# Values of the first group of heads for the last two token blocks by Strassen's scheme

## The chip, the cores and the metric

The kernel runs on one core of a Trainium2 chip. The metric is the device time of one execution in microseconds (us). TensorE does the matrix products, VectorE (DVE in the profile) and ScalarE (ACT) the elementwise work, GpSimd (POOL) and SyncE (SP) mostly issue transfers. Everything is float32.

## The reference

One transformer block over 2048 tokens of width 512, with modulation vectors made from a conditioning row `c`:

```
mod = silu(c) @ wmod                      # sa, ca, ga, sb, cb, gb, each 512 wide
h   = layernorm(x) * (1 + ca) + sa
q, k, v = h @ Q_w + Q_b, h @ K_w + K_b, h @ V_w + V_b      # 16 heads of 128
scores  = softmax(causal(q @ k.T / sqrt(128)))
x   = x + ga * ((scores @ v) @ O_w + O_b)
h   = layernorm(x) * (1 + cb) + sb
x   = x + gb * (top-4-of-64 expert FFN(h) + 2 shared experts(h))
```

Only the product `h @ V_w` is touched here, for heads 0 and 1 and for tokens 1024 to 2047.

## The kernel before

**Layout.** The normalised tokens are kept transposed in four blocks of 512 tokens, `hTs[0]` to `hTs[3]`, each 128 partitions x 4 chunks of the width x 512 tokens. For each pair of blocks `b` there are four differences of their halves, `Ts[b]`, made once by `sum_h(b)` on VectorE. They serve a scheme of Strassen's kind (seven products in place of eight) that already makes the queries and keys of heads 1 to 15 (`project`) and the values of head groups 1 to 7 (`values`, L434 to L487). A head group is two heads; group 0 is heads 0 and 1.

**Two ways to make values.** `make_v(g, t)` (L489 to L504) makes the values of both heads of a group for one tile of 128 tokens: four matmuls with 256 moving columns into one PSUM tile, tag "mm", and one ScalarE copy out of it (L504). Eight such calls make two token blocks. `values(g, b, s)` makes the same two token blocks in seven steps. Each step is one product of eight matmuls with 128 moving columns (four token tiles, two chunks of the width, L447) into one PSUM tile of the same tag, and one or two evictions: the first product goes by a ScalarE copy (L461) into a buffer `p_`, and the others are added into `u` or into the value tiles by VectorE (L464 to L483, seven additions, the fourth step having two). The scheme needs sums of the group's weights, which `value_sums(g)` writes into `sgb` by four VectorE additions of 128x256 (L428 to L431). The tag "mm" has two PSUM buffers, so a product can begin when the eviction of the last but one is done.

A matmul of the source is two TensorE instructions in the profile, so a call of `make_v` shows as 8 instructions of 256 columns and a product of `values` as 16 of 128 columns, each with a weight load of 128x128 beside it (PEld).

**Order.** The attention runs as a list of steps (head, batch); each head has five batches of pairs of token tiles, `BATCHES = ((7,), (6,), (5, 0), (4, 1), (3, 2))`. For a batch, `softmax_work` gives chunks of up to 1024 keys: matmuls into `ps` (L572), a causal mask (L584) and the row maximum (L585, L589) on VectorE, the exponential on ScalarE (L591, L601), and a scaling by the row sums (L550 to L554 on VectorE, then L559 or L795). `swap` sends the probabilities through 16 transfers issued by SP (L616), `turn` transposes 32x32 blocks on VectorE (L626, four per batch), and `weighted_values` multiplies with the values (L644).

Ahead of the loop over the steps there is a prologue (L818 to L826), which has no `weighted_values` yet. It merges the softmax chunks of the first two batches of head 0 with other products as filler: the values of group 0 and the last three query blocks of head 0 (`plain`, L170, evicted by ScalarE at L177). The helper `merge(streams, marks)` writes the engines' instructions in an order fixed at build time: it always takes the next item from the stream that is least advanced by its share of columns, and calls a mark's function when the given share of all columns is done. Each engine then runs its own list in that order.

```python
work = softmax_work(0) + softmax_work(1)
fill = [(1024, lambda t=t: make_v(0, t)) for t in range(NT)]
fill += [(2048, lambda j=j: plain(0, j, qts[0, j])) for j in (2, 0, 1)]
merge([work[:4], fill[:8]], [])
swap(0)
marks = [(at, lambda a=a: turn(0, a)) for a, at in enumerate((0.55, 0.65, 0.75, 0.85))]
merge([work[4:], fill[8:]], marks)
swap(1)
```

In what follows, chunks 1 to 4 are those of the first batch (pair 7) and chunks 5 to 8 those of the second (pair 6).

Of the kernel before, what the change touches and what calls it, by code (L numbers as in the profile page):

```python
# [23 lines left out]
def adaln_block_kernel(  # L24
# [30 lines left out]
    NT = N // P  # L55
# [22 lines left out]
    sgb = const.tile([P, 2, D], F32)  # L78
# [6 lines left out]
    def merge(streams, marks):  # L85


        totals = [sum(c for c, _ in s) for s in streams]
        whole = sum(totals)
        done = [0] * len(streams)  # L90
        at = [0] * len(streams)
        marks = sorted(marks, key=lambda m: m[0])
        while True:
            ready = [i for i, s in enumerate(streams) if at[i] < len(s)]
            while marks and (not ready or sum(done) >= marks[0][0] * whole):
                marks.pop(0)[1]()
            if not ready:
                break
            i = min(ready, key=lambda i: (done[i] / totals[i], i))
            c, f = streams[i][at[i]]  # L100
            f()
            done[i] += c
            at[i] += 1
# [19 lines left out]
    with ExitStack() as att:  # L123
# [41 lines left out]
        def plain(b, j, dst):  # L165

            w = heads[0][b]
            ps = psA.tile([P, 512], F32, name="pqk", tag="mm")
            for k in range(DC):
                nc.tensor.matmul(  # L170
                    out=ps,
                    lhsT=w[:, k, :],
                    rhs=hTs[j][:, k, :],
                    start=(k == 0),
                    stop=(k == DC - 1),
                )
            nc.scalar.activation(  # L177
                dst, ps, AF.Identity, bias=qkb[:, b, 0:1], scale=scale if b == 0 else 1.0
            )
# [245 lines left out]
        def value_sums(g):  # L425
            wv = groups[g]
            s = sgb.rearrange("p a (j k d) -> p (a j) k d", j=2, k=2)
            nc.vector.tensor_add(s[:, 0], wv[:, 0:2, 1], wv[:, 2:4, 1])  # L428
            nc.vector.tensor_sub(s[:, 1], s[:, 0], wv[:, 0:2, 0])
            nc.vector.tensor_sub(s[:, 2], wv[:, 0:2, 0], wv[:, 0:2, 1])  # L430
            nc.vector.tensor_sub(s[:, 3], wv[:, 2:4, 0], s[:, 1])  # L431
            return s
# [56 lines left out]
        def make_v(g, t):  # L489

            if t % 4 == 0:
                at = vplace[g][t // 4]
                vts[g, t // 4] = vp.tile([P, 4, HG * DH], F32, name=f"v{at}")
            wv = groups[g]
            ps = psA.tile([P, HG * DH], F32, name="pv", tag="mm")
            for k in range(DC):
                nc.tensor.matmul(  # L497
                    out=ps,
                    lhsT=hTs[t // 4][:, k, (t % 4) * P : (t % 4 + 1) * P],
                    rhs=wv[:, k].rearrange("p i d -> p (i d)"),  # L500
                    start=(k == 0),
                    stop=(k == DC - 1),
                )
            nc.scalar.copy(vts[g, t // 4][:, t % 4, :], ps)  # L504
# [295 lines left out]
        def softmax_work(n):  # L800
            hd, s = steps[n]
            probs[n] = pp.tile([P, PW], F32, name="p")
            tiles = {}
            for pr, i, _ in CHUNKS[s]:
                if (pr, i) not in tiles:
                    tiles[pr, i] = softmax_tile(hd, s, pr, i, probs[n])
            assert sum(len(chunks) for chunks in tiles.values()) == len(CHUNKS[s])
            return [tiles[pr, i][c] for pr, i, c in CHUNKS[s]]

        def swap(n):  # L810
            flush()
            flush_shares()
            turned[n] = swap_blocks(steps[n][1], probs.pop(n))

        def turn(n, a):
            turn_blocks(steps[n][1], turned[n], a)

        with tc.manual_schedule():  # L818
            work = softmax_work(0) + softmax_work(1)
            fill = [(1024, lambda t=t: make_v(0, t)) for t in range(NT)]  # L820
            fill += [(2048, lambda j=j: plain(0, j, qts[0, j])) for j in (2, 0, 1)]
            merge([work[:4], fill[:8]], [])
            swap(0)
            marks = [(at, lambda a=a: turn(0, a)) for a, at in enumerate((0.55, 0.65, 0.75, 0.85))]
            merge([work[4:], fill[8:]], marks)
            swap(1)  # L826
            outs = []
            for n, (hd, s) in enumerate(steps):
                if s == 3:
                    if hd + 2 < H:  # L830
                        heads[hd + 2] = load_head(hd + 2)
                    if hd % HG == 1 and hd // HG + 2 < NG:
                        groups[hd // HG + 2] = load_group(hd // HG + 2)
                fill = fillers(hd, s)
                if (hd, s) in MOD_LOADS:
                    load_mod(MOD_LOADS[hd, s], hd // HG)
                if (hd, s) in MOD_ROWS:
                    fill.append((2048, lambda m=MOD_ROWS[hd, s]: late_mod(*m)))
                if (hd, s) in ((2, 3), (15, 2)):
                    mag = qkw.tile([P, 512], F32, name="p_")  # L840
                    gate(mag, ga if hd == 2 else gb)
                if (hd, s) == (14, 0):
                    nc.sync.dma_start(out=sgb, in_=modd.partition_broadcast(P))
                if (hd, s) == (14, 1):
                    fill.insert(2, (0, lambda: load_wo(0)))
                if (hd, s) == (14, 2):
                    load_wo(1)
                    load_ab(0, heads=((0, 4), (4, 8)))
                if (hd, s) == (14, 3):
                    load_wo(2)  # L850
                    load_ab(0, heads=((8, 12), (12, 14)))
                    first, second = [
                        vow.tile([P, DC, HG, DH], F32, name="wv").rearrange("p k i d -> p (k i d)")
                        for _ in range(2)
                    ]
                    parts += [first[:, :D], first[:, D:], second[:, :D]]
                    last3 = second[:, D : D + (NE - 1) * P]
                if (hd, s) == (14, 4):
                    load_wo(3)
                    load_ab(0, heads=((14, 15),))  # L860
                    for u in range(NE):
                        load_x_tile(u)
                    rest = spare(hd // HG)
                    nc.sync.dma_start(out=rest[0][:, :D], in_=O_b.partition_broadcast(P))
                    for u in range(NE):
                        outs += begin_output(u)
                if hd == H - 1 and s == 0:
                    load_ab(1, heads=((0, 4), (4, 8)))
                if hd == H - 1 and s == 1:
                    load_ab(1, heads=((8, 12), (12, 15)))  # L870
                if hd == H - 1 and s == 2:
                    load_ab(2)
                if hd == H - 1 and s == 4:
                    nc.vector.tensor_copy(ga, rest[0][:, D:])
                    nc.sync.dma_start(out=last3, in_=atd[H - 1, :, : (NE - 1) * P])
                    nc.sync.dma_start(out=ones, in_=atd[H - 1, :, (NE - 1) * P : NE * P])
                if outs:
                    upto = 8 if hd < H - 1 else (14, 14, 14, 10)[s]
                    fill += outs[:upto]
                    del outs[:upto]  # L880
                streams = [fill, weighted_values(hd, s, turned.pop(n))]
                if n + 2 < len(steps):
                    streams.insert(0, softmax_work(n + 2))
                marks = [(f, lambda i=i: scale_wo(i)) for f, i in WO_SCALES.get((hd, s), ())]
                if s == 4 and hd + 2 < H:
                    marks.append((0.05, lambda: scale_w(hd + 2)))
                    marks.append((0.3, lambda: sum_w(hd + 2)))
                if n + 1 < len(steps):
                    for a, at in enumerate((0.58, 0.66, 0.8, 0.88)):
                        marks.append((at, lambda a=a: turn(n + 1, a)))  # L890
                merge([st for st in streams if st], marks)
                if n + 2 < len(steps):
                    swap(n + 2)
            assert not outs and not ahead
# [273 lines left out]
    with ExitStack() as ex:  # L1168
# [346 lines left out]
        with tc.manual_schedule():  # L1515
# [13 lines left out]
            for n, (_, f) in enumerate(tail):  # L1529
                f()  # L1530
                upto = min(NT, READY[n])
                while done < upto:
                    t = order[done]
# [37 lines left out]
```

## Time and profile before

| | us |
|---|---|
| median of 3 runs | 2372.84 (2370.08 to 2377.7) |
| the profiled execution's own time | 2360.04 |
| its span, first to last instruction | 2358.2 |
| mean granted TensorE clock | 0.998 of full speed |

The profile and the trace are of that one execution, whose span leaves 1.8 us of its time around it. It ran 12.8 us faster than the median of the runs that are timed, so a sum of durations is compared with its own 2360.04 us, and the difference is then carried over to the median. In the span TensorE is busy 99%, VectorE 66%, ScalarE 36%; the busy time of TensorE is modelled from the starts of its instructions. A group or a row of the timeline gives start and duration in us, engine, line, operation, output and input tile, size and count, and in brackets the idle time of the engine ahead of it with what ended it.

### The profile page before, as it was taken

To read this page: it belongs to the slowest core of one execution; us is meant where nothing else is said; L and a number is where in the kernel's file an instruction comes from. 1 tells how busy PE (TensorE), PEld (TensorE's weight loads), DVE (VectorE), ACT (ScalarE), POOL (GpSimd) and SP (SyncE) were. 2 spreads that over 40 slices of the span, in tenths; PEclk is the share of its full clock that TensorE was granted. 3 is DMA by queue.
4 is the path that set the end of the run, shared out by engine and by line. 5 is a ranking of instruction groups with operands and counts; after the bars stand their busy time and mean duration, and the time that the engine had idled before them with its cause. 6 is when DMAs were issued, how large, how long until landed. Compare 5 with 4: busy or idle time off the path is not lost.

```text
span 2358.2 us, 27676 instructions
## 1 busy us (share of the span) xinstructions
PE 2332.4 (99%) x9078; PEld 1505.0 (64%) x9078; DVE 1547.3 (66%) x3100; ACT 860.2 (36%) x1703; POOL 218.2 (9%) x286
## 2 busy tenths in 40 slices
PE   7999999999999999999999999999999999999999
PEld 3666667666676676766766757555544576877743
DVE  5467767677776777767767777764844663644664
ACT  3444444444444444444444444432211222222200
POOL 0000000000000000000000000000000111111073
PEclk9999999999999999999999999999999999999999
DMA  4234544454454454454545545675332478778665
GB/s 143 57 87 117 126 120 117 99 144 114 98 141 97 115 122 97 117 122 105 126 98 127 121 98 136 174 195 150 123 120 89 132 222 242 229 211 251 183 202 157
DMA packets 223836, 325.84 MB, mean 138 GB/s; under 512 B 31895, under 2 KB 138443, under 8 KB 223693
## 3 DMA queue, kind: packets, MB, share of 16 engines
q1 hardware_dynamic: 196812, 252.74, 41.8%
q0 software_dynamic: 17664, 54.54, 7.8%
q10 hardware_dynamic: 9216, 16.78, 1.9%
q8 instruction: 73, 1.20, 0.2%
q14 instruction: 71, 0.57, 0.1%
HBM read 139.39 MB, written 41.95 MB: 77 GB/s over the span
## 4 chain that ended last, share of the span: by engine, by line
PE 85%; SPq 4%; DVE 3%; DMA 2%; issue 1%; ACT 1%; POOL 0%; ACTq 0%; DVEq 0%; POOLq 0%
PE po L644 17%; PE ps L572 16%; PE pqk L222 14%; PE pso L1140 7%; PE pv L447 5%; PE pst L1289 5%; PE pse L1433 5%; PE psd L1351 5%; SPq L616 4%; PE psy L1454 2%; PE psb L769 2%; PE psg L1205 2%; PE tpx L1426 1%; PE pv L497 1%; DVE nm L585 1%
## 5 line engine op out<-in xcount | busy, mean ns | idle before, releaser
L591 ACT ACTIVATE p<-ps,nm 128x1024 f32<-128x1024 f32 (+7 forms) x384 | 331.5, 863 | 837.3 <-DVE nm L585 344.7
L644 PE MATMUL po<-pt,v 128*128 128x256 f32 (+1 forms) x2304 | 564.5, 368 | 3.0 <-DVE pt L626 2.3
L644 PEld LDWEIGHTS po<-pt,v 128*128 128x128 f32 x2304 | 422.6, 191 | 214.0 <-issue 164.3
L572 PE MATMUL ps<-kt,qt 128*128 128x512 f32 (+3 forms) x1280 | 528.8, 530 | 1.2 <-ACT qt L177 0.8
L585 DVE TENSOR_REDUCE nm<-ps 128x1 f32<-128x1024 f32 (+7 forms) x384 | 350.0, 911 | 111.9 <-PE ps L572 103.1
L626 DVE STREAM_TRANSPOSE pt<-pt 128x832 f32<-128x832 f32 (+2 forms) x320 | 337.4, 1070 | 21.2 <-DMA pt<-p 18.1
L572 PEld LDWEIGHTS ps<-kt,qt 128*128 128x128 f32 x1280 | 232.9, 191 | 154.4 <-issue 136.2
L795 ACT ACTIVATE p<-p,rs 128x1024 f32<-128x1024 f32 (+4 forms) x320 | 266.0, 860 | 5.4 <-DVE rs L554 5.1
L658 POOL DMA_DIRECT2D atd<-at x128 | 74.5, 586 | 1566.7 <-ACT at L653 1544.2
L1140 PE MATMUL pso<-hT,T 128*128 128x512 f32 x384 | 173.7, 598 | 0.0
L222 PE MATMUL pqk<-T,sw 128*128 128x512 f32 x360 | 169.2, 593 | 0.0
L584 DVE TENSOR_TENSOR ps<-ps,causal 128x128 f32<-128x128 f32 x256 | 72.6, 284 | 96.1 <-PE ps L572 93.8
L1433 PE MATMUL pse<-wgu,xbT 128*128 128x256 f32 x512 | 121.1, 380 | 0.0
L1140 PEld LDWEIGHTS pso<-hT,T 128*128 128x128 f32 x384 | 69.7, 191 | 71.4 <-issue 70.4
L222 PE MATMUL pqk<-hT,wq 128*128 128x512 f32 x240 | 112.8, 593 | 0.0
L1351 PE MATMUL psd<-wsd,hs 128*128 128x512 f32 x256 | 111.5, 593 | 0.0
L222 PEld LDWEIGHTS pqk<-T,sw 128*128 128x128 f32 x360 | 68.6, 191 | 53.9 <-issue 50.1
L1433 PEld LDWEIGHTS pse<-wgu,xbT 128*128 128x128 f32 x512 | 94.0, 191 | 11.5 <-issue 1.0
L1416 POOL DMA_INDIRECT xb<-h2d,tok x64 | 65.0, 1016 | 297.8 <-PE tpx L1426 275.3
L1428 ACT COPY xbT<-tpx 128x512 f32<-128x512 f32 x64 | 37.3, 585 | 145.8 <-DVE y L1456 56.2
L447 PEld LDWEIGHTS pv<-sgb,T 128*128 128x128 f32 x672 | 81.7, 192 | 8.1 <-issue 6.7
L1351 PEld LDWEIGHTS psd<-wsd,hs 128*128 128x128 f32 x256 | 48.7, 191 | 58.9 <-issue 58.0
(423 smaller groups left out, 2646.8 us busy)
## 6 DMA issues: line engine op xcount, KB each, us to landing
pt<-p SPq DMA_DIRECT2D x768, 104.0 KB, 2.2
pt<-p SPq DMA_DIRECT2D x256, 124.0 KB, 2.3
pt<-p SPq DMA_DIRECT2D x256, 108.0 KB, 2.2
atd<-at POOLq DMA_DIRECT2D x128, 128.0 KB, 2.2
wgu<-in_L_ffn_Wg_dram SPq DMA_DIRECT2D x64, 256.0 KB, 4.6
wgu<-in_L_ffn_Wu_dram SPq DMA_DIRECT2D x64, 256.0 KB, 4.6
wd<-in_L_ffn_Wd_dram SPq DMA_DIRECT2D x64, 256.0 KB, 4.0
ybd<-y ACTq DMA_DIRECT2D x64, 256.0 KB, 3.8
```

Of the source, the lines that this page charges most:

```text
L222: nc.tensor.matmul(out=ps, lhsT=l[:, k], rhs=r[:, k], start=(k == 0), stop=(k == 1))
L447: nc.tensor.matmul(out=ps[:, n], lhsT=l[:, k, n * P : (n + 1) * P], rhs=r[:, k], start=(k == 0), stop=(k == 1),)
L572: nc.tensor.matmul(out=ps[:, o : o + wo], lhsT=q, rhs=kts[hd, (c0 + o) // 512][:, :wo], start=True, stop=True,)
L585: nc.vector.tensor_reduce(nm[:, n : n + 1], ps[:, :w], AX.X, ALU.max, negate=True)
L591: nc.scalar.activation(rows[:, r0 + c0 // P : r0 + (c0 + w) // P], ps[:, :w].rearrange("q (r b k) -> q r b k", b=4, k=32), AF.Exp, bias=nm ...
L626: nc.vector.transpose(part, part)
L644: nc.tensor.matmul(out=po if wide else po[:, P:], lhsT=vts[g, kt // 4][:, kt % 4, hh * DH : (hh + 1) * DH], rhs=rows[:, r : r + last + 1 : ...
L795: nc.scalar.activation(part, part, AF.Identity, scale=r)
L1140: nc.tensor.matmul(out=ps, lhsT=abs_[pr][:, hd, i * P : (i + 1) * P], rhs=wos[hd // 4][:, hd % 4, :], start=(hd == 0), stop=(hd == H - 1),)
L1289: nc.tensor.matmul(out=ps[:, h], lhsT=w[:, k, :], rhs=x_[:, k, :], start=k == 0, stop=k == 1,)
L1351: nc.tensor.matmul(out=ps, lhsT=hsh[b, f][:, i * P : (i + 1) * P], rhs=wsd[:, f, :], start=(f == 0), stop=(f == NHC - 1),)
L1433: nc.tensor.matmul(out=ps, lhsT=xts[e][:, k, :], rhs=weights[e][:, k].rearrange("p i h -> p (i h)"), start=(k == 0), stop=(k == DC - 1),)
```

## The change

The values of group 0 for tokens 1024 to 2047 are made by `values(0, 1, ...)` and no longer by eight calls of `make_v`. The weight sums of group 0 are written at a mark 0.7 of the way through the first merge. Nothing else in the source differs.

```diff
             work = softmax_work(0) + softmax_work(1)
-            fill = [(1024, lambda t=t: make_v(0, t)) for t in range(NT)]
+            fill = [(1024, lambda t=t: make_v(0, t)) for t in range(NT // 2)]
+            fill += values(0, 1, sgb.rearrange("p a (j k d) -> p (a j) k d", j=2, k=2))
             fill += [(2048, lambda j=j: plain(0, j, qts[0, j])) for j in (2, 0, 1)]
-            merge([work[:4], fill[:8]], [])
+            merge([work[:4], fill[:8]], [(0.7, lambda: value_sums(0))])
             swap(0)
             marks = [(at, lambda a=a: turn(0, a)) for a, at in enumerate((0.55, 0.65, 0.75, 0.85))]
             merge([work[4:], fill[8:]], marks)
```

In the order of the built programs the engines' lists differ in one stretch only, from the end of chunk 3 to chunk 8:

- TensorE: behind chunk 5 (the first of the second batch, L572 at 77.51 us) come four products of `values` in place of five calls of `make_v`, then chunk 6, then three products in place of three calls, then chunk 7. From there on the list is the same.
- VectorE: four sums (L428 to L431) ahead of the mask of chunk 4; the evictions L464, L468, L473, L474 between the maximum of chunk 5 and the mask of chunk 6; L477, L480, L483 between the maxima of chunks 6 and 7. The first of the four transposes of the first batch (L626) stands behind the maximum of chunk 7 and no longer behind that of chunk 6, directly ahead of the second and third.
- ScalarE: one copy of 128x512 (L461) behind the exponential of chunk 5, and eight copies of 128x256 (L504) fewer.
- The lists of SP and GpSimd are the same.

The step functions of `values` (cut):

```python
def first():
    box["p"] = qkw.tile([P, 512], F32, name="p_")...
    nc.scalar.copy(box["p"], product(hTs[i][:, 0:2], wv[:, 0:2, 0]))
def second():
    nc.vector.tensor_add(u, box["p"], product(T[:, 1], s[:, 1]))
def third():
    nc.vector.tensor_add(of(i, 1), u, product(T[:, 2], s[:, 2]))
def fourth():
    ps = product(T[:, 0], s[:, 0])
    nc.vector.tensor_add(of(j, 1), of(i, 1), ps)
    nc.vector.tensor_add(of(j, 0), u, ps)
def fifth():
    nc.vector.tensor_sub(of(i, 1), of(i, 1), product(T[:, 3], wv[:, 2:4, 1]))
def sixth():
    nc.vector.tensor_add(of(j, 0), of(j, 0), product(hTs[j][:, 2:4], s[:, 3]))
def seventh():
    nc.vector.tensor_add(of(i, 0), box["p"], product(hTs[i][:, 2:4], wv[:, 2:4, 0]))
```

## The prediction

> **What bounds the kernel now.** I read the shares of the engines first, then the busy time by stages, then the timeline of the stage that is changed. TensorE is the bound:
>
> ```profile
> PE 2332.4 (99%) x9078; PEld 1505.0 (64%) x9078; DVE 1547.3 (66%) x3100; ACT 860.2 (36%) x1703; POOL 218.2 (9%) x286
> ```
>
> The table by stages (length, then busy us of PE, PEld, DVE, ACT, POOL) cuts the prologue at chunk 5 and at the first matmul of the step loop:
>
> ```profile
> 77.50:111.80 34.30, 33.65 (x114) 21.10 (x113) 15.08 (x26) 12.93 (x28) 0.00 (x0) 1.00 0.30 66
> 111.80:800.00 688.20, 687.81 (x2805) 458.75 (x2804) 495.07 (x937) 311.48 (x604) 32.70 (x56) 1.00 0.48 116
> 800.00:1500.00 700.00, 699.95 (x2853) 467.65 (x2852) 510.36 (x967) 326.31 (x632) 33.02 (x57) 1.00 0.48 115
> ```
>
> In the changed stage (first row) TensorE stands 0.65 us of 34.30, and VectorE is busy 15.08 us, ScalarE 12.93. The other two rows say what becomes of a gain: for nearly 1400 us behind it TensorE has 0.44 us without work, so no later wait can swallow a microsecond, and what starts earlier ends earlier. The timeline of TensorE in the stage, with ScalarE's rows that release it:
>
> ```profile
> 77.51 1.88 PE L572 MATMUL ps<-kt,qt 128*128 128x512 f32 x4
> 79.23 3.62 PE L497 MATMUL pv<-wv,hT 128*128 128x256 f32 x16
> 83.50 5.45 PE L497 MATMUL pv<-wv,hT 128*128 128x256 f32 x24 [0.65 <-ACT v L504]
> 88.78 1.45 PE L572 MATMUL ps<-kt,qt 128*128 128x512 f32 x4
> 90.07 5.34 PE L497 MATMUL pv<-wv,hT 128*128 128x256 f32 x24
> 95.25 1.02 PE L572 MATMUL ps<-kt,qt 128*128 128x512 f32 x2
> ...
> 81.98 1.11 ACT L591 ACTIVATE p<-ps,nm 128x1024 f32<-128x1024 f32 x1 [2.94 <-DVE nm L585]
> 82.99 0.19 ACT L591 ACTIVATION_READ_ACCUMULATOR p<-ps,nm 128x1 f32 x1
> 83.08 0.64 ACT L504 COPY v<-pv 128x256 f32<-128x256 f32 x2
> ```
>
> The reader is to see the one stall. The third call needs the PSUM buffer of the first, whose copy stands in ScalarE's list behind the exponential of chunk 5, and that ends only at 83.08. TensorE goes on at 83.50.
>
> **Removed.** Eight calls of `make_v`. Three run from 90.07 to 95.25, start to start, so one is 5.18 / 3 = 1.727 us and eight are 13.81. Eight copies of 0.37 us leave ScalarE, which waits there anyway.
>
> **Added on TensorE.** Seven products. The same product is in the trace in every later group, first at 169.04, between other work:
>
> ```profile
> 169.04:170.82 1.78, 1.78 (x17) 1.78 (x16) 1.02 (x4) 1.78 (x4) 0.00 (x0) 1.00 0.00 0
> ```
>
> That is 1.78 us from start to start, and the weight loads fill all of it (PEld 1.78 too, 16 loads). Seven are 7 x 1.78 = 12.46. So an eighth of the columns goes, but not an eighth of the time. The gain is 13.81 - 12.46 = 1.35 us. What the trace doesn't show is several products in a row, as there will be here. From below, a product costs the pace of the wider matmuls, 1.727: gain 1.72. From above, loads that no matmul hides (first rival). I take 1.78, the row of the same operation; its loads already follow each other without a gap.
>
> **The wait at the third product.** The first two products run from 79.23 to 82.79. The third needs the first's buffer, and so the copy into `p_`, which stands where the old copy stood: 83.08, but 128x512 for 128x256. The trace has that copy at 0.58 us (173.65, L461). It ends at 83.66, and the third product starts 0.05 later as now (83.45 to 83.50): 83.71. TensorE stands 83.71 - 82.79 = 0.92 us, where start to start it now stands 83.50 - 79.23 - 2 x 1.727 = 0.82. Loss 0.10. Bounds: 0 if the copy starts earlier, 0.6 if the release is late by another such copy.
>
> **The other evictions.** They are seven VectorE additions; the same rows elsewhere in the trace take 0.65 to 0.69 us, 4.8 in all, beside 15.08 busy of 34.30. One by one, from 83.71 and with 0.2 us from a product's end to its reader (chunk 7's matmuls give way to the next at 96.97, and its maximum starts at 97.17):
>
> - L464 waits on VectorE for `p_` (83.66) and ends by 84.45; the fourth product needs that buffer at 85.49. Slack 1.0. Behind it in VectorE's list stands only the next eviction and the mask of chunk 6, for which nothing is ready before 88.5.
> - L468 ends at 86.4, wanted by the fifth product at 88.56 (fourth until 87.27, then chunk 6, 1.29). Slack 2.2.
> - L473 and L474 end at 88.8, wanted at 90.34. Slack 1.5. The mask of chunk 6 starts right behind them, as its matmuls end.
> - The maximum of chunk 6 (0.30 + 0.96 + 0.16, from 88.8) is over at 90.2, so L477 runs 90.54 to 91.2, wanted by the seventh product at 92.12. Slack 0.9, the smallest.
> - L480 and L483 end by 93.0 and 94.8; the first two `plain` blocks want these buffers at 95.7 and 99.1.
>
> So they cost nothing as long as VectorE is no more than 0.9 us late; beyond it every microsecond is one.
>
> **The sums.** Four additions, 169.84 to 171.30 where the trace has them, 1.46 us. They stand ahead of the mask of chunk 4, where VectorE is idle:
>
> ```profile
> 75.79 0.30 DVE L584 TENSOR_TENSOR ps<-ps,causal 128x128 f32<-128x128 f32 x1 [3.21 <-PE ps L572]
> ...
> 97.17 1.23 DVE L585 TENSOR_REDUCE nm<-ps 128x1 f32<-128x1024 f32 x1 [4.18 <-PE ps L572]
> 98.93 2.31 DVE L626 STREAM_TRANSPOSE pt<-pt 128x992 f32<-128x992 f32 x2
> 105.12 0.30 DVE L584 TENSOR_TENSOR ps<-ps,causal 128x128 f32<-128x128 f32 x1 [3.88 <-PE ps L572]
> ```
>
> They fit into the 3.21 us with 1.7 over: cost nothing. Without that cover they would hold chunk 4's maximum for up to 1.46. Their weights landed long before.
>
> **The moved transpose.** It runs just ahead of the other two, 1.21 + 2.31 = 3.5 us from about 97.7 to 101.2, and the mask of chunk 8 then comes at 103.9. Slack 2.7. The fourth and the values' first matmul (now 111.78) keep their distance, since both hang on chunk 8. No transfer and no queue is passed.
>
> **Sum.** -13.81 + 12.46 + 0.10 = -1.25 us: chunk 7 starts at about 94.0 for 95.25, and everything behind it is as much earlier. Against the profiled execution 2360.04 - 1.25 = 2358.8; against the median, which is 12.8 higher, 2372.84 - 1.25 = 2371.6. That is 0.05%, and a measurement of this kernel can tell about 0.3% (7.1 us) from no change.
>
> **Rivals.**
>
> *Weight loads come into the open (slower).* The stage then has 7 x 16 = 112 loads for 8 x 8 = 64, and one load takes 191 ns in its rows. A 256-column matmul hides it, a 128-column one barely. If in long rows of products the 48 further loads no longer overlap, they cost 48 x 0.191 = 9.2 us: 2371.6 + 9.2 = 2380.8, slower by 0.34%. From one load in seven in the open (1.25 of 9.2) the change is slower than before, from nine in ten by over 0.3%. For it: PEld is full for a whole product. Against: in that row 16 loads and 16 matmuls both fit into 1.78 us. The Trainium skill has a rule that speaks against the change ("TensorE: Matmul & The Clock Gate", Part 3, The mechanism): a weight load overlaps a running matmul only if it goes to other row groups, and these loads use all 128 rows. By it, and by that page's load time of P / 1.2, an estimate is 48 x 107 ns = 5.1 us more, 2376.7. The row above, with both in 1.78 us, disagrees. Chance 0.05.
>
> *Evictions through VectorE set the pace.* Two products wait for a VectorE that is busy with a maximum (1.23) and a mask (0.30) each, beyond the slack of 0.9: up to 2 x 1.5 = 3.0, 2374.6. For it: seven evictions change to an engine with longer work in its list. Against: the slacks above. It decides from 0.9 us of lateness. Chance 0.07.
>
> *The gain doesn't reach the end.* Some transfer in the loop holds TensorE at a fixed time: 2372.8. Against: 0.44 us of idle TensorE in 1388. Chance 0.08.
>
> That the change doesn't do what it says can be left out: the order of the built program has the seven products in place of the eight calls.
>
> **How the numbers follow.** 0.80 is left for the forecast. Executions of one program differ by more than any of these terms: the three runs lie 7.6 us apart, the profiled one 10 below them, so I let a median be off by some 5 us either way. Range: the forecast less 6.1, 2365.5, to the eviction rival plus 3.4, 2378.0; the exposed loads stay outside. Faster by over 0.3% (under 2365.7) needs 5.9 us of such scatter: 0.09. Slower (over 2380) needs 8.4 of it, 0.03, or the exposed loads, 0.05: 0.08. Within: 0.83.
>
> **What would show it.** Right: L447 in seven groups of about 1.78 us from 79.2; one wait ahead of the third, near 0.9, put down to ACT `p_` L461 or DVE; chunk 7 near 94.0; the step loop's first L644 near 110.5; span near 2357. Wrong: a pace of L447 above 0.115 us in rows of 32 or 48; a further idle row of PE on DVE L464 to L480; chunk 7 early but the loop's later landmarks (L447 at 169.04) not 1.25 earlier. A difference of several microseconds that sits behind 112 us and has no row in this stage would refute the whole reading.

## The result and the profile after

| | before | changed | ratio, 95% interval |
|---|---|---|---|
| median of 20 runs each, us | 2373.89 (2370.08 to 2377.7) | 2371.67 (2367.36 to 2375.46) | 0.9988 (0.9983 to 0.9994) |
| profiled execution, us | 2360.04 | 2368.66 | |
| its span, us | 2358.2 | 2366.9 | |

The medians say 2.2 us less; 2371.6 was predicted. The interval leaves out 1, so the changed kernel is faster, by 1.4 to 4.0 us, though by less than the 0.3% that the prediction took for the least that can be told apart. The two profiled executions say 8.6 us more. The traces show where that comes from: a stage that the change doesn't touch.

The timeline of TensorE in the changed stage, changed kernel (start, duration, engine, line, operation, tiles, size, count, and in brackets the idle time with its releaser):

```profile
76.49 1.88 PE L572 MATMUL ps<-kt,qt 128*128 128x512 f32 x4
78.21 1.95 PE L447 MATMUL pv<-wv,hT 128*128 128x128 f32 x16
80.00 1.95 PE L447 MATMUL pv<-sgb,T 128*128 128x128 f32 x16
82.69 3.84 PE L447 MATMUL pv<-sgb,T 128*128 128x128 f32 x32 [0.75 <-ACT p__561 L461]
86.37 1.46 PE L572 MATMUL ps<-kt,qt 128*128 128x512 f32 x4
87.66 1.95 PE L447 MATMUL pv<-wv,T 128*128 128x128 f32 x16
89.44 1.95 PE L447 MATMUL pv<-sgb,hT 128*128 128x128 f32 x16
91.23 1.95 PE L447 MATMUL pv<-wv,hT 128*128 128x128 f32 x16
93.02 1.88 PE L572 MATMUL ps<-kt,qt 128*128 128x512 f32 x4
```

The reader is to see one bracket, ahead of the third product, and a pace of 1.78 to 1.79 us from product to product wherever one follows another without a wait. (The two behind the wait take 3.68 us, 0.1 more than two paces. The kernel before has the same 0.1 behind its wait: three calls take 5.28 us from 83.50 and 5.18 from 90.07.) From chunk 5 to chunk 7 it is 93.02 - 76.49, 16.52 us before rounding; before it was 95.25 - 77.51 = 17.74. Chunk 5 itself starts 1.02 us earlier, because everything ahead of chunk 1 (54.15 for 55.17) happened to be shorter. The later landmark, the values of the next group, moved by both: 166.80 for 169.04 is 2.24 = 1.02 + 1.22.

The wait ends with these rows of ScalarE, where the copy into `p_` (L461) stands right behind the exponential of chunk 5 (L591):

```profile
80.96 1.11 ACT L591 ACTIVATE p<-ps,nm 128x1024 f32<-128x1024 f32 x1 [2.93 <-DVE nm L585]
81.97 0.19 ACT L591 ACTIVATION_READ_ACCUMULATOR p<-ps,nm 128x1 f32 x1
82.06 0.58 ACT L461 COPY p__561<-pv 128x512 f32<-128x512 f32 x1
```

The rows that show whether VectorE and ScalarE held anything up:

```profile
71.47 0.42 DVE L428 TENSOR_TENSOR sgb<-wv 128x256 f32<-128x256 f32 x1
71.92 0.42 DVE L429 TENSOR_TENSOR sgb<-sgb,wv 128x256 f32<-128x256 f32 x1
72.27 0.42 DVE L430 TENSOR_TENSOR sgb<-wv 128x256 f32<-128x256 f32 x1
72.60 0.42 DVE L431 TENSOR_TENSOR sgb<-wv,sgb 128x256 f32<-128x256 f32 x1
74.77 0.30 DVE L584 TENSOR_TENSOR ps<-ps,causal 128x128 f32<-128x128 f32 x1 [1.75 <-PE ps L572]
...
82.67 0.69 DVE L464 TENSOR_TENSOR cb<-p__561,pv 128x512 f32<-128x512 f32 x1 [1.75 <-ACT p__561 L461]
84.78 0.69 DVE L468 TENSOR_TENSOR v<-cb,pv 128x512 f32<-128x512 f32 x1 [1.43 <-PE pv L447]
...
89.64 0.69 DVE L477 TENSOR_TENSOR v<-v,pv 128x512 f32<-128x512 f32 x1 [0.30 <-PE pv L447]
...
96.70 3.40 DVE L626 STREAM_TRANSPOSE pt<-pt 128x992 f32<-128x992 f32 x3
102.88 0.30 DVE L584 TENSOR_TENSOR ps<-ps,causal 128x128 f32<-128x128 f32 x1 [2.79 <-PE ps L572]
```

The sums leave 1.75 us of idle VectorE behind them. Ahead of L468 and L477 it is VectorE that waits for TensorE and not the other way round; L477 is over at 90.33, 0.90 us before the seventh product. The moved transpose leaves 2.79 us ahead of chunk 8's mask.

By stages (length, then busy us of PE, PEld, DVE, ACT, POOL, then the granted clock):

```profile
77.50:111.80 34.30, 33.55 (x169) 22.82 (x168) 19.67 (x33) 11.25 (x22) 0.00 (x0) 1.00 0.34 77
111.80:800.00 688.20, 688.20 (x2808) 458.67 (x2807) 497.95 (x944) 312.88 (x605) 32.69 (x56) 1.00 0.48 116
800.00:1500.00 700.00, 699.89 (x2852) 466.50 (x2851) 508.22 (x963) 323.55 (x628) 33.55 (x58) 1.00 0.48 115
```

Up to 1500 us TensorE has 0.11 us without work in 1388 behind the stage, so the gain has nothing to be lost in there. When the last stage begins, in which the shared experts run and GpSimd gathers the experts' rows, the changed execution is 4.1 us ahead: the 1.02 and the 1.22, and 1.85 from the step loop, whose lists are the same in both (from the first L644 to the last 1526.79 us for 1528.64). What made the profiled execution longer is the last stage. From its first matmul to the end of the span it takes 2366.9 - 2239.28 = 127.6 us, for 2358.24 - 2243.42 = 114.8 before. The longest waits of TensorE in it, changed kernel:

```profile
2287.88 5.40 PE L1206 MATMUL psg<-h2T,wsu 128*128 128x512 f32 x8 [3.80 <-DVE sig L1195]
2299.16 5.39 PE L1206 MATMUL psg<-h2T,wsg 128*128 128x512 f32 x8 [5.88 <-DVE hs L1196]
```

### The profile page after: what moved, and what is told of

Read it like the earlier page. It is cut to its first block, busy times and chain, and to the rows that moved or that the text cites. A ratio compares the mean times of both kernels' runs of the same rounds, so it can differ in the third digit from the quotient of the medians.

```text
span 2366.9 us, 27781 instructions
## 1 busy us (share of the span) xinstructions
PE 2332.4 (99%) x9126; PEld 1503.7 (64%) x9126; DVE 1551.9 (66%) x3111; ACT 858.4 (36%) x1696; POOL 218.1 (9%) x286
## 4 chain that ended last, share of the span: by engine, by line
PE 92%; DVE 2%; SPq 1%; issue 1%; another core or an unknown queue 1%; ACT 1%; DMA 0%; DVEq 0%; ACTq 0%
PE po L644 19%; PE ps L572 19%; PE pqk L222 15%; PE pv L447 7%; PE pso L1141 7%; PE pst L1290 5%; PE pse L1434 5%; PE psd L1352 4%; PE psg L1206 3%; PE psy L1455 2%; PE psb L769 2%; PE tpx L1427 1%; SPq L616 1%; PE pl L983 1%
## 5 line engine op out<-in xcount | busy, mean ns | idle before, releaser
L591 ACT ACTIVATE p<-ps,nm 128x1024 f32<-128x1024 f32 (+7 forms) x384 | 331.9, 864 | 842.7 <-DVE nm L585 348.0
L644 PE MATMUL po<-pt,v 128*128 128x256 f32 (+1 forms) x2304 | 564.0, 368 | 2.6 <-DVE pt L626 1.8
L644 PEld LDWEIGHTS po<-pt,v 128*128 128x128 f32 x2304 | 421.6, 190 | 214.3 <-issue 164.8
L572 PE MATMUL ps<-kt,qt 128*128 128x512 f32 (+3 forms) x1280 | 528.2, 529 | 0.9 <-ACT qt L177 0.8
L626 DVE STREAM_TRANSPOSE pt<-pt 128x832 f32<-128x832 f32 (+2 forms) x320 | 337.1, 1069 | 19.6 <-DMA pt<-p 17.1
L572 PEld LDWEIGHTS ps<-kt,qt 128*128 128x128 f32 x1280 | 232.3, 190 | 153.4 <-issue 136.7
L1434 PE MATMUL pse<-wgu,xbT 128*128 128x256 f32 x512 | 121.1, 379 | 0.0
L447 PEld LDWEIGHTS pv<-sgb,T 128*128 128x128 f32 x720 | 87.2, 192 | 9.1 <-issue 6.7
L447 PE MATMUL pv<-sgb,T 128*128 128x128 f32 x720 | 87.6, 275 | 0.7 <-ACT p__561 L461 0.7
## 6 DMA issues: line engine op xcount, KB each, us to landing
atd<-at POOLq DMA_DIRECT2D x128, 128.0 KB
```

The lines of the kernel that those rows point to most:

```text
L447: nc.tensor.matmul(out=ps[:, n], lhsT=l[:, k, n * P : (n + 1) * P], rhs=r[:, k], start=(k == 0), stop=(k == 1),)
L572: nc.tensor.matmul(out=ps[:, o : o + wo], lhsT=q, rhs=kts[hd, (c0 + o) // 512][:, :wo], start=True, stop=True,)
L591: nc.scalar.activation(rows[:, r0 + c0 // P : r0 + (c0 + w) // P], ps[:, :w].rearrange("q (r b k) -> q r b k", b=4, k=32), AF.Exp, bias=nm ...
L626: nc.vector.transpose(part, part)
L644: nc.tensor.matmul(out=po if wide else po[:, P:], lhsT=vts[g, kt // 4][:, kt % 4, hh * DH : (hh + 1) * DH], rhs=rows[:, r : r + last + 1 : ...
L1434: nc.tensor.matmul(out=ps, lhsT=xts[e][:, k, :], rhs=weights[e][:, k].rearrange("p i h -> p (i h)"), start=(k == 0), stop=(k == DC - 1),)
```

## The experiments

**Theory.** The stage gives 1.2 us, made up as predicted (seven products for eight calls, with a wait of 0.9 in place of 0.8), and all of it reaches the end; the last stage differs between executions whatever the values do. **Rivals.** Weight loads or the sums cost something that the profile doesn't show; the median's 2.2 us is something else than the stage's 1.2; the long last stage comes from the change.

Four chips were used, each in one session, with the kernel before on each: its median was 2374.25 us on the first, 2373.72 on the second, 2359.78 on the third and 2360.65 on the fourth. For every run the table gives three stretches of its profiled execution: chunk 1 to chunk 5, chunk 5 to chunk 7, and the last stage.

| run | chip | median, us | ratio to before (95%) | 1 to 5 | 5 to 7 | last |
|---|---|---|---|---|---|---|
| before, profile of the start | | | | 22.34 | 17.74 | 114.8 |
| changed, profile of the result | | | | 22.34 | 16.52 | 127.6 |
| changed, again | 1 | 2372.20 | 0.9991 (0.9982 to 1.0000) | 22.34 | 16.53 | 129.4 |
| sums only | 1 | 2373.76 | 0.9999 (0.9990 to 1.0008) | 22.35 | 17.74 | 130.0 |
| first copy on VectorE | 1 | 2370.37 | 0.9988 (0.9979 to 0.9997) | 22.35 | 15.51 | 129.6 |
| products done twice | 1 | 2382.62 | 1.0036 (1.0023 to 1.0050) | 22.35 | 28.02 | 130.1 |
| 64 columns | 2 | 2385.35 | 1.0043 (1.0028 to 1.0058) | 22.34 | 31.54 | 129.8 |
| both pairs | 2 | 2364.89 | 0.9959 (0.9946 to 0.9973) | 19.26 | 15.55 | 128.0 |
| changed, three gather buffers | 2 | 2364.86 | 0.9961 (0.9948 to 0.9975) | 22.35 | 16.53 | 121.1 |
| changed, two gather buffers | 2 | 2368.85 | 0.9979 (0.9969 to 0.9989) | 22.34 | 16.53 | 123.6 |
| both pairs, three gather buffers | 3 | 2353.75 | 0.9974 (0.9964 to 0.9984) | 19.26 | 15.55 | 115.9 |
| before, three gather buffers | 3 | 2360.79 | 1.0002 (0.9993 to 1.0011) | 22.34 | 17.74 | 115.6 |
| changed, third time | 4 | 2358.90 | 0.9992 (0.9983 to 1.0001) | 22.34 | 16.52 | 116.4 |
| both pairs, again | 4 | 2354.39 | 0.9973 (0.9962 to 0.9984) | 19.26 | 15.55 | 118.0 |

**The changed kernel again.**

> The changed kernel a second time. Theory A (the gain is the 1.25 us of the changed stage and nothing else): chunk 5 to chunk 7 takes 16.5 us again (before 17.74), the ratio to the kernel before is near 0.9995. Theory B (something behind the stage, in the step loop, gains 1 to 2 us more in every execution): the ratio is near 0.9988 again, and from the first matmul L644 of the loop to its last the trace takes about 1526.8 us, as in the first trace of the change, not 1528.65 as in the one before. Theory C (the prologue's neighbours): the stretch before chunk 5 differs too.

The stage repeats to 0.01 us. The median is 2.05 us below the kernel before of the same chip, between the two theories' ratios. The step loop takes 1527.9 us, neither the 1526.8 of theory B nor the 1528.65 of before.

**The sums alone**, in the kernel before:

```diff
-            merge([work[:4], fill[:8]], [])
+            merge([work[:4], fill[:8]], [(0.7, lambda: value_sums(0))])
```

> The kernel before with only the four weight sums added at the same mark; the values are still made by the calls of make_v. Theory A: the sums run while VectorE waits for chunk 4, chunk 5 to chunk 7 takes 17.74 us as before, ratio 1.0000. Rival (the sums delay the mask of chunk 4): up to 1.46 us more ahead of chunk 5. Its step loop has the same lists as before: if L644 first to last takes 1528.6 us in this trace too, the 1.9 us shorter loop of the change is systematic; if it lies anywhere between 1526.5 and 1529, it is scatter of single executions.

No stretch of the stage moved, and neither did the median (0.5 us less). The sums cost nothing that shows. The step loop takes 1528.9 us, which by the terms above could be either a property of the kernel or scatter; it is taken up below.

**The first product copied by VectorE**, in the changed kernel:

```diff
-                nc.scalar.copy(box["p"], product(hTs[i][:, 0:2], wv[:, 0:2, 0]))
+                if g == 0:
+                    nc.vector.tensor_copy(box["p"], product(hTs[i][:, 0:2], wv[:, 0:2, 0]))
+                else:
+                    nc.scalar.copy(box["p"], product(hTs[i][:, 0:2], wv[:, 0:2, 0]))
```

> The change with the first product of group 0 copied out of PSUM by VectorE in place of ScalarE (one line). VectorE is free behind the maximum of chunk 5 (79.71 + 1.22 in the trace of the change), so the copy ends some 0.7 us later, near 81.6, ahead of the end of the second product (81.78). Theory A: the wait of 0.75 to 0.92 us ahead of the third product is gone, chunk 5 to chunk 7 takes 15.6 us, and the ratio falls by 0.0004 against the change alone. Rival (VectorE in the chain sets the pace): the wait moves to the fourth or fifth product and the stretch stays at 16.5.

The timeline of TensorE:

```profile
78.66 1.95 PE L447 MATMUL pv<-wv,hT 128*128 128x128 f32 x16
80.45 5.52 PE L447 MATMUL pv<-sgb,T 128*128 128x128 f32 x48
```

Three products run on without the bracket, and the stage is 1.02 us shorter. So the wait was the copy's place behind the exponential in ScalarE's list, and the evictions on VectorE bear one more without holding TensorE up.

**The products' matmuls done twice for group 0** (the second pass begins its sums anew, `start=(k == 0)`, so the values stay what they were):

```diff
-                for n in range(4):
+                for n in [n for _ in range(2 if g == 0 else 1) for n in range(4)]:
```

> The change with the matmuls of each of the seven products of group 0 done twice into the same PSUM tile; nothing is added on other engines. A dose on TensorE alone: 7 x 1.78 = 12.46 us. Theory A (every microsecond of this stage is carried to the end): chunk 5 to chunk 7 takes some 29 us less what the longer products hide of the wait ahead of the third (0.9), and the time is 11.5 to 12.5 us over that of the change, ratio to before 1.0037 to 1.0048. Rival (the gain or loss is swallowed behind the stage): the stage is as much longer but the ratio stays under 1.002. Weight loads that come into the open in rows of 16 matmuls and more: over 1.78 us for a product, 2.2 at the half of 48 further loads exposed.

The stage grew by 11.50 us. Seven further products of 1.787 are 12.51; the wait of 0.90 ahead of the third is covered by the longer second product, which leaves 11.6. The median grew by 10.4 over the changed kernel on the same chip. A cost put into this stage comes out at the end nearly whole, so a gain should too. In rows of 96 (10.72 us until chunk 6 starts) a pair of load and matmul still takes 0.112 us.

**Narrower matmuls, four times as many loads**: the kernel before, `make_v` for the last eight tiles in four pieces of 64 columns: 8 x 32 = 256 loads in place of 64, for the same columns.

```diff
+            pieces = 4 if t >= NT // 2 else 1
+            w = HG * DH // pieces
+            for c in range(pieces):
                 for k in range(DC):
                     nc.tensor.matmul(
-                        out=ps,
+                        out=ps[:, c * w : (c + 1) * w],
...
-                        rhs=wv[:, k].rearrange("p i d -> p (i d)"),
+                        rhs=wv[:, k].rearrange("p i d -> p (i d)")[:, c * w : (c + 1) * w],
```

> The kernel before, with each of the eight calls of make_v for tokens 1024 to 2047 done in four column pieces of 64: the same columns in all, but 16 matmuls of the source and so 32 instructions and 32 weight loads per call, where it had 8. It measures the price of a weight load that the columns cannot hide. Theory A (a load takes a slot of 0.1115 us, as in a product of values, and a matmul of 128 columns hides no more than that): a call takes 32 x 0.1115 = 3.57 us, and chunk 5 to chunk 7 grows from 17.74 by 8 x 1.84 = 14.7 less the 0.8 of the copy's wait that longer calls hide, to some 31.6. Rival (loads are free beside matmuls): 17.74. Rival (a load costs its full row of 191 ns once it is not hidden): 32 x 0.191 = 6.1 us a call, the stretch is over 50 us.

The timeline of TensorE:

```profile
78.33 17.98 PE L500 MATMUL pv<-wv,hT 128*128 128x64 f32 x160
96.14 1.51 PE L575 MATMUL ps<-kt,qt 128*128 128x512 f32 x4
97.49 10.83 PE L500 MATMUL pv<-wv,hT 128*128 128x64 f32 x96
```

160 matmuls of 64 columns take 96.14 - 78.33 = 17.81 us, 0.1113 each: as much as one of 128 columns (1.787 / 16 = 0.1117), where one of 256 takes 5.18 / 24 = 0.216. So a load and its matmul together are not shorter than 0.111 us here, and a 128-column matmul lies just at that floor: its load is hidden, and nothing is left over. Whether the load or the matmul sets the floor isn't told apart, since both became four times as many. The prediction cited a rule against the change (the Trainium skill, "TensorE: Matmul & The Clock Gate", Part 3, The mechanism): a load overlaps a running matmul only on other row groups. The same section also lets a load run ahead into a background weight buffer. By the rule and that page's 107 ns a load (P / 1.2), with the columns' time behind it (half of 0.216), an estimate for a pair would be 0.215 us. The traces do not agree: these loads use all 128 rows, and a pair takes half of that. At the end the run is 11.6 us longer (6.6 to 13.8 by the interval), for 13.8 in the stage.

**Strassen's scheme for all four blocks**, with the sums ahead of chunk 1 and the second pair's first product copied by VectorE:

```diff
+            wv0 = groups[0]
+            s0 = sgb.rearrange("p a (j k d) -> p (a j) k d", j=2, k=2)
+            nc.vector.tensor_add(s0[:, 0], wv0[:, 0:2, 1], wv0[:, 2:4, 1])
...
-            fill = [(1024, lambda t=t: make_v(0, t)) for t in range(NT)]
+            fill = values(0, 0, s0) + values(0, 1, s0)
...
-            merge([work[:4], fill[:8]], [])
+            merge([work[:4], fill[:7]], [])
...
```

> The same scheme for all four token blocks of group 0: the sums stand ahead of the sums for head 1 in the prologue, values(0, 0) takes the place of the first eight calls of make_v, and the first product of the second pair is copied by VectorE. Theory A: the stretch from chunk 1 to chunk 5 falls from 22.34 to some 19.3 (1.35 for the products, and the 1.3 us that the third call waits now, since chunk 2 then stands ahead of the third product), chunk 5 to chunk 7 is 15.5 as in e3; the time is 5 us under the kernel before, ratio 0.9979. Rival (VectorE is not free there: it makes the sums of the last two token blocks until 61.4): the first stretch stays over 21.

The stretches gave 3.08 + 2.19 = 5.27 us, the median 8.8 (6.4 to 12.8 by the interval), so 3.5 us are not from these stretches; the last stage of this execution is 1.8 us shorter than that of the 64-column run on the same chip, and the run on the fourth chip below gives 6.3. The 3.08 are the exchange of eight calls for seven products (1.30) and, for the rest, waits that are gone; most of that stands in one row of TensorE's waits in the changed kernel, whose wait of 1.3 us the kernel before has too and this one has not:

```profile
PE pv L497 <- ACT v L504: 1.3, 1, 1.3
```

**Fewer buffers for the gathered rows.** In the long last stages the updates of TensorE's semaphore came late. In the changed kernel's profile the matmul chains of L1206 ended at 2280.65 and 2293.28 and their updates were recorded at 2286.48 and 2298.39, 5.8 and 5.1 us later; in before's profile the lag of every such update was 0.02. VectorE waits for these updates, then TensorE for VectorE. In that time GpSimd issues a gather about every 1.25 us without a pause, and the update of 2298.39 came in the first long pause between gathers (2297.2 to 2302.4, for a free buffer), though the one of 2286.48 came without a pause. In the runs changed again, sums only and both pairs, too, the most delayed update came in the first pause (in that of both pairs 2281.26, in a pause from 2277.6 to 2285.3). Fewer buffers should make pauses earlier:

```diff
-        ygp = ex.enter_context(tc.tile_pool(name="ygp", bufs=4, side="right"))
+        ygp = ex.enter_context(tc.tile_pool(name="ygp", bufs=3, side="right"))
```

> The change with 3 buffers in place of 4 for the rows that the last stage gathers (yg); nothing else differs, and no list of an engine does. In the traces so far the stage from the last shared unit to the end takes 127.6 to 130.1 us where the trace of before has 114.8, and in the long ones a VectorE or ScalarE instruction waits 3 to 16 us for an update of TensorE's semaphore whose matmul has long ended, while GpSimd issues gathers without a pause; the update comes when GpSimd has to wait for a buffer. Theory T (the unbroken row of gathers holds TensorE's updates back): with less lead GpSimd pauses earlier, the waits get shorter and the stage falls under 122. Rival (the rows arrive late, or the lateness has another cause): 127 or more.

> As e7 with 2 buffers. Theory T: shorter waits again, unless the gathers (four a tile, 1.25 us each, and 4 to 5 us to land) then come too late for VectorE, which would show as waits of acc L1498 for yg. Last stage 115 to 122. Rival: 127 or more.

Three buffers shortened the last stage from 128 to 130 to 121.1 us, two to 123.6, over the 122 that both were to stay under, and the medians lie 8.9 and 4.9 us below the kernel before, of which about 2 are the change's own. With three buffers TensorE still waits once, 4.5 us; with two VectorE waits 13.7 us in all for gathered rows, for 5.9 with three. So fewer buffers help on this chip. That it is the pauses which let the updates through is argued and not shown: with two buffers there is one about every 7 us from 2249 to 2264, and the updates are on time until 2274, but with three the late updates of 2275.89 and 2283.08 came shortly ahead of the pauses (from 2277.5 and 2284.6), and on the chips below the updates are on time without any pause. Why they are late stays open.

**The two together, and the buffers without the change.** On a third chip:

> Strassen's scheme for all four token blocks of group 0, the second pair's first product copied by VectorE, and three buffers for the gathered rows of the last stage in place of four. If the gains of the two earlier runs come from different stages they add: 19.3 us from chunk 1 to chunk 5 and 15.5 to chunk 7, a tail near 121 us, and a median near 2357 (8.8 for the values and 6.8 for the buffers below 2372). If the 8.8 of the run with both pairs was partly scatter and only the 5.2 us that its stages show is real, near 2360. If the shorter tail was chance, 2365.

> The kernel before with three buffers for the gathered rows in place of four, nothing else. If the tail is independent of the changed stage, it is near 121 us, the changed stage keeps its 17.74, and the median lies 6 to 7 us below the kernel before, near 2366.5, and some 1.2 to 2 us above the changed kernel with three buffers (2364.9). If the gain of the three buffers hangs on the change, it stays at 2373.

The kernel before needs 2359.78 here, and its last stage is short with three buffers (115.6). Three buffers gain nothing (1.0002). So what they cured is not in every chip, or not in every session. With both pairs the gain is 6.0 us, for 5.27 in the stretches, and 2353.75 is the lowest median of all. TensorE in it, from just behind chunk 1 to chunk 5 and from there to the step loop's first matmul:

```profile
55.20:73.75 18.55, 18.55 (x127) 15.14 (x127) 15.19 (x24) 7.63 (x11) 0.00 (x0) 1.00 0.00 1
73.75:105.84 32.09, 32.09 (x163) 21.52 (x162) 21.01 (x36) 10.01 (x19) 0.00 (x0) 1.00 0.31 71
```

TensorE has no idle time left in either.

**The changed kernel and both pairs on a fourth chip**, with four buffers:

> The changed kernel once more. The step is 1.22 us in the changed stage wherever it runs (16.52 for 17.74). If the kernel before needs about 2360 on this chip, its last stage is short (near 115 us) in both kernels, the executions scatter less, and the difference of the medians should be nearer to the stage's own 1.2 than the 2.2 seen so far. If it needs about 2374, the last stage is near 128 in both, and the difference lies between 0 and 4.

> Strassen's scheme for all four token blocks, as run before, with four buffers in the last stage. The stages give 5.3 us (19.26 for 22.34 and 15.55 for 17.74). On a chip with the short last stage the median should lie 5 to 6.5 us below the kernel before, as it did with three buffers (6.0); on one with the long stage, 5 to 9 as in its first run.

This chip too has the short last stage. The changed kernel is 1.75 us below the kernel before, both pairs 6.3. TensorE's longest wait for the shared experts is now

```profile
PE psg L1206 <- DVE sig L1195: 1.9, 2, 1.8
```

although the gathers follow each other there as closely as in the long stages (0.30 us between them).

## Why the prediction was right, step by step

- **Removed and added.** Right. Seven products at 1.787 measured are 12.51 for 12.46; in rows of 32, 48 and 96 the pace doesn't change, which was the unknown.
- **The wait at the third product.** Right: 82.69 - 80.00 - 1.79 = 0.90 us from start to start, predicted 0.92. That it is the copy's place in ScalarE's list is shown by the run that moves the copy.
- **Evictions, sums, moved transpose at nothing.** Right: the smallest slack, at L477, was worked out as 0.9 and measures 0.90; the one behind the moved transpose as 2.7 and measures 2.79. No wait of TensorE on VectorE is in this stage.
- **The sum.** -1.25 predicted, -1.22 (-1.21 to -1.22 in three executions) measured from chunk 5 to chunk 7. Chunk 7 stands at 93.02 for the 94.0 named, since the stretch ahead of chunk 1 was 1.02 shorter.
- **Reaching the end.** Right as far as the runs go: 11.50 us put into the stage gave 10.4 at the end, 13.80 gave 11.6, and a gain of 5.27 gave 6.0 and 6.3 on the chips with the short last stage, and 8.8 on one with the long. All of these ends, and those of the change itself, lie some 0.5 to 3.5 us on the fast side of what the stage says.
- **The size at the end.** The medians moved by 2.2, 2.05 and 1.75 us, the stage by 1.22. By the first interval (4.0 to 1.4 us) the two don't quite meet, by the other two they do. So that 2371.6 meets 2371.67 is in part luck: the base of the prediction was 2372.84, from three runs, and is 2373.89 over twenty, and the drop is 2.2 for the 1.25 forecast. The remaining 0.5 to 1.0 us stays open. The stretch ahead of chunk 1 may hold some of it: its mean is 54.9 us over four executions with the old values (54.27 to 55.22) and 54.4 over seven with the new ones (54.13 to 54.97), but the two overlap, and nothing ahead of chunk 1 differs in the engines' lists. The step loop may hold some too. The prediction's table ends at 1500 us; the longest wait of TensorE in the loop comes behind it, near 1530 (before, then changed):

```profile
PE po L644 <- DVE pt L626: 2.3, 1, 2.3
PE po L644 <- DVE pt L626: 1.8, 1, 1.8
```

This wait is 2.1 to 2.4 us in the three executions with the unaltered calls of `make_v` (before, sums only, before with three buffers) and 1.5 to 1.8 in the eleven others. It is also short in the run with 64 columns, which has no product of the scheme there, so a shorter wait doesn't need the scheme. Other waits scatter against it: the loop takes 1527.3 to 1528.9 us in those three, 1526.8 to 1528.0 in the five with the changed kernel's lists, 1526.3 to 1526.8 in the three with both pairs. That is an order by kernel, with overlaps; its cause is not shown, and no run tested it.

- **The base.** The offset of 12.8 us between profile and median was carried over as a constant, which was right for the difference, without its cause being known. It is the last stage, and it goes with the chip (or its session): 2373.72 and 2374.25 us on two, 2359.78 and 2360.65 on two others, where the last stages with four buffers are 10 to 15 us shorter. That before's profile was taken on a chip of the second kind is inferred from its time, which lies 10 us below the lowest of the twenty runs before. The prediction's own criterion, a span near 2357, therefore failed in the result's profile (2366.9) and is met on the fourth chip (2356.9). By its last criterion a difference of several microseconds behind 112 us would refute the whole reading. The last stage is such a difference, 12.8 us; it does not refute the reading of the changed stage, since the last stage is long without the change (130.0, sums only) and short with it (116.4, fourth chip).
- **The rivals.** Weight loads in the open: refuted by the pace above. Evictions setting the pace: refuted. Gain not reaching the end: refuted by the doubled products.

## What to carry to other kernels

Cutting columns by an eighth can pay an eighth only while a matmul is well above the floor of a load and its matmul (0.111 us here); at half the width, which lies at that floor, the eighth gave 9.4% (1.30 us of 13.81), and a wait of 0.9 us beside it could be taken away by giving one copy to another engine. Compare a profile and a median only when both are from one chip, and compare kernels by stretches between landmarks: a change of 1.2 us was exact in its stage, while the whole executions differed by 8.6 the other way. An edit that pays on one chip, such as the buffer count here, should be run on a second before it is kept.

## What the runs showed of the hardware

- A 128x128 float32 load with its matmul takes 0.111 us at 64 columns, 0.112 at 128, and 0.216 at 256. The same page of the Trainium skill (Part 2, Back-to-back issue gap) says that the spacing of such pairs is set by both operations and gives 81 ns for 128 columns. This kernel's float32 pairs show 0.112, and the measurement decides.
- On two of four chips updates of TensorE's semaphore were recorded microseconds after the end of their matmuls while GpSimd issued indirect gathers without a pause, and VectorE waited for them: 15.7 us in the second run of the changed kernel (2275.18 to 2290.91, and a wait of TensorE of 12.8 us), 17.0 in that of both pairs (2264.31 to 2281.26). On the two others the same gathers left them 0.02 us late in the executions profiled. What differs between the chips is not shown.
- The waits of TensorE bring a second cost, in the row of this stretch of the changed kernel's profile (its eighth column is the granted clock):

```profile
2280.00:2300.00 20.00, 10.32 (x19) 4.05 (x18) 5.55 (x9) 0.60 (x1) 13.24 (x14) 0.81 0.75 222
```

In the trace the granted clock falls to half twice, 1.1 us behind the end of the first wait for 3.4 us, and 2.5 us into the second wait for 6.8 us; in before's trace, and in that of the fourth chip's changed kernel, it stays at 1.00 from 35 us to 2355. The rows of eight matmuls there take 5.40 and 5.39 us for the 3.60 of the others. The two waits, 9.7 us, and these 3.6 us make up the 12.8 us by which the stage is longer than in before's profile, which has a wait of 0.4 in it.
